# A Perceiver layer pair on one core: another order of loads at the start, another first expert, and causal weights zeroed on GpSimd

## The chip, the core and the metric

The kernel runs on one core of one Trainium2 chip. The metric is the device time of one execution in microseconds. An execution under the profiler has a time of its own, and its span (first to last instruction) is a little shorter than that time.

## The reference

The input is a latent x of 512 tokens by 512 features, a context of 8192 tokens by 512 features, and a mask over the context. Two layers follow each other, and each adds three blocks to x in turn. All have 16 heads of 32 features.

- Cross attention: layer norm of x, queries from it, keys and values from the context, a softmax over the context tokens that the mask leaves, an output projection. In layer 0 queries and keys are normalised per head.
- Self attention over the 512 tokens. In layer 0 a score counts only where the key's position is not before the query's:

```python
scores = jnp.where(j >= i, scores, -jnp.inf)
attn = jax.nn.softmax(scores, axis=-1)
```

  In layer 1 each query sees a window of neighbours.
- A mixture of 8 experts. A router picks two experts for each token, and the gated sum of their answers is added. The hidden width is 2048 in layer 0 and 1024 in layer 1.

## The kernel before, in words

Everything is float32, with small bfloat16 products where a mask or a shift is added to scores. The program is written against a framework that schedules: it gives every DMA one of eight semaphore lanes for each kind of queue in turn, makes a DMA wait until the last user of its lane has landed, and arranges each engine's instructions by when it expects them to be ready. [...]

**Opening.** Constants are built on GpSimd (POOL): masks, counters, and `rooms`, which hold each expert's capacity and first row. The key mask (`c8`) is turned into a short list `irow` of at most 15 context tiles that hold an unmasked token (`tile_list`). SP reads this list into registers (L609) and then issues the context tiles (`cslot`, L620), two to a slot, four slots at once. Ahead of that SP loads x in four pieces, the query weights `wq`, and the broadcast biases `bq` and `bkf`; ACT loads the key and value weights `wkvf` in four pieces. `columns` (L935) loads a vector of 512 numbers as 128 x 4, through ACT's queue; `padded_columns` (L1242) loads a key bias in four pieces, through SP's queue. `columns_of` uses both and scales the query bias on POOL (L943). `clear_answers` writes zeros into `answers_d`, the DRAM buffer for the experts' answers, with nine stores of 256 KB and a small one through POOL's queue (L84, L85). `aside`, called in the fourth step of the key loop, holds the output bias, those zeros and the columns for the next blocks, but the scheduler may issue them earlier.

**Cross attention (layer 0).** Layer norm (`lnt` is its transposition on TensorE), values of four tiles (`pv`), queries (`qps`), and then a loop over the 15 tiles: keys (`pk`), their normalisation, the transposition (`ktp`), running maxima of scores. A scan of the other mask runs beside it: SP loads pieces `mi`, POOL reads the first column of each (`first`), ACT squares differences (`square`). Then a long loop of scores, exponentials and weighted sums, kept ahead by the maxima of the next group of heads.

**Self attention (layer 0).** Four groups of four heads. For each group four steps, from the last block of 128 keys to the first, with 512, 384, 256 and 128 queries. A first pass (`M` in a hand-written order of steps) takes maxima, a second (`W`, function `weighted`) subtracts them by a small product, takes exponentials into `pT`, and `sums` multiplies the last step's `pT` with values (`acc`) and with ones (`den`). In both passes a bfloat16 product of `negi` (minus a huge number on the diagonal) with `before` (one where the key is before the query) is added to the diagonal block of scores (L1314). `F` finishes a group; the last group is finished by query block (`E`, `T`).

**Experts.** Experts are ranked by how many tokens chose them; rank r has room for `CAPS[r]` tokens, and the products for it have that many columns. `by_rank` finds the rank of each expert (`erank`), and `has` marks which expert stands in which place. The loop goes through the places in order, in `n` chunks of 512 hidden features (4 in layer 0, 2 in layer 1): `hidden` (`hps`), the activation, `back` (`y`). SP issues two weights of 1 MB for each chunk, four buffers each. Tokens of the first place are gathered by products with a one-hot matrix (`gather`, `gps`, L1737). For the others, a list of tokens (`lists`, `token_of`) is made and POOL gathers blocks of 128 rows from DRAM (`xrows`, L1751), which TensorE transposes (`xtp`, L1759). The loop asks for the blocks that the second place needs in its chunk before the last of the first place:

```python
if i % n == n - 2 and r + 1 < E:
    while waiting and waiting[0][0] * P < starts[r + 1] + caps[r + 1]:
        waiting.pop(0)[1]()
        fetch()
```

## Time and profile before

| | |
|---|---|
| time, median of 3 runs | 1718.99 us (1718.89 to 1719.83) |
| the profiled execution: its own time | 1715.68 us |
| its span | 1713.8 us |
| mean granted TensorE clock | 0.941 |
| TensorE (PE) busy | 1566.6 us, 91% |
| VectorE (DVE) / ScalarE (ACT) / GpSimd (POOL) busy | 45% / 33% / 25% |
| first value product on TensorE | at 28.24 us |
| causal self attention | about 556 to 650 us |
| experts of layer 0 / layer 1, first product of the gather | at 670.46 us / 1515.61 us |

A line of the timeline gives the start, the duration, the engine, the source line, the operation with output and inputs, and in brackets the engine's idle time before it with what ended it. SPq, ACTq and the like are DMA issues. A line of the windows gives a stretch, then for PE, PEld (TensorE's weight loads), DVE, ACT and POOL the busy time with the count of instructions, then the granted TensorE clock, the share of the DMA engines' time and GB/s. A group has busy time and mean duration, then idle time before it.

### The profile page before, as it was taken

What the parts mean: (1) busy time and instruction counts of PE and PEld (TensorE: products, weight loads), DVE (VectorE), ACT (ScalarE), POOL (GpSimd) and SP (SyncE); (2) the same over time, 40 slices, a digit from 0 to 9 for tenths busy, and PEclk for the clock granted to TensorE, in tenths of its full rate; (3) what the DMA queues carried; (4) which work ended last, traced back from release to release, by engine and by line L of the source; (5) the groups of instructions that cost most, each with busy time, mean ns of one, the idle gap of its engine ahead of it and who ended that gap; (6) DMA issues with size and microseconds to landing.
All of it is one profiled execution on the core that took longest, in us unless ns stands there. A gap on an engine that the chain in (4) does not pass through costs nothing. (4 is left out here: it accounts for less than half of the span.)

```text
span 1713.8 us, 24266 instructions
## 1 busy us (share of the span) xinstructions
PE 1566.6 (91%) x9933; PEld 914.2 (53%) x9933; DVE 775.0 (45%) x1394; ACT 569.5 (33%) x1079; POOL 424.9 (25%) x306
## 2 busy tenths in 40 slices
PE   3889999999979997999999799999999989679996
PEld 2333333333234446999999465433333245369995
DVE  5366677774633645111112233567765536831112
ACT  1366445556622132111111211165556612211110
POOL 4000057788110001000002100068776110010002
PEclk9999989999989977999999899999999989879997
DMA  7055200000030003878885400000000040064672
GB/s 247 24 161 178 74 1 1 1 1 1 1 129 1 1 1 134 311 265 286 282 295 171 155 25 19 25 1 1 1 1 1 1 151 10 15 224 171 219 265 90
DMA packets 87144, 168.79 MB, mean 98 GB/s; under 512 B 8450, under 2 KB 23842, under 8 KB 85600
## 3 DMA queue, kind: packets, MB, share of 16 engines
q1 hardware_dynamic: 78352, 147.87, 25.4%
q0 software_dynamic: 5440, 17.01, 2.8%
q10 hardware_dynamic: 3216, 2.11, 0.4%
q8 instruction: 84, 1.38, 0.3%
q14 instruction: 52, 0.43, 0.1%
HBM read 156.30 MB, written 9.63 MB: 97 GB/s over the span
## 5 line engine op out<-in xcount | busy, mean ns | idle before, releaser
L869 ACT ACTIVATE pT<-sc,kbias 128x512 f32<-128x512 f32 x480 | 299.1, 686 | 205.1 <-PE sc L639 142.4
L752 PE MATMUL sc<-qTf,kTf 32*128 32x512 f32 x1264 | 297.0, 653 | 6.4 <-DVE d L861 4.9
L765 DVE SCALAR_TENSOR_TENSOR mx<-scm,kbias,mx 128x512 f32<-128x512 f32 x312 | 215.4, 743 | 97.8 <-PE scm L752 95.5
L752 PE MATMUL scm<-qTf,kTf 32*128 32x512 f32 x656 | 240.8, 653 | 2.1 <-DVE mx L765 2.1
L1790 PE MATMUL y<-hT,w 128*128 128x160 f32 (+13 forms) x1536 | 212.3, 298 | 2.4 <-DVE hT L1965 2.3
L1790 PEld LDWEIGHTS y<-hT,w 128*128 128x128 f32 x1536 | 205.1, 197 | 4.4 <-DVE hT L1965 2.8
L1774 PE MATMUL hps<-tokens,w 128*128 128x160 f32 (+13 forms) x1536 | 207.0, 293 | 0.0
L1774 PEld LDWEIGHTS hps<-tokens,w 128*128 128x128 f32 x1536 | 198.7, 192 | 1.8
L842 POOL TENSOR_TENSOR four<-four,pT 128x2048 f32<-128x2048 f32 x42 | 190.6, 4538 | 9.7 <-ACT pT L869 6.7
L752 PEld LDWEIGHTS sc<-qTf,kTf 32*128 32x128 f32 x1264 | 90.6, 189 | 148.4 <-issue 111.9
L842 POOL TENSOR_TENSOR four<-pT 128x2048 f32<-128x2048 f32 x24 | 109.0, 4542 | 109.2 <-ACT pT L869 109.2
L824 PE MATMUL acc<-pT,vNf 128*32 128x512 f32 x960 | 133.8, 624 | 1.5 <-ACT o L831 1.5
L765 DVE SCALAR_TENSOR_TENSOR mx<-sc,kbias,mx 128x512 f32<-128x512 f32 x136 | 93.3, 744 | 79.8 <-PE sc L752 79.8
L1965 DVE TENSOR_TENSOR hT<-sg,hps 128x320 f32<-128x320 f32 (+7 forms) x64 | 27.9, 436 | 189.5 <-ACT sg L1964 189.5
L752 PEld LDWEIGHTS scm<-qTf,kTf 32*128 32x128 f32 x656 | 75.0, 188 | 49.8 <-DVE mx L765 38.0
L639 PE MATMUL sc<-shift,ones 3*128 3x512 bf16 (+3 forms) x544 | 100.2, 383 | 0.0
L1815 POOL DMA_DIRECT2D answers_d<-yb x17 | 9.4, 556 | 291.7 <-ACT yb L1808 291.7
L1964 ACT ACTIVATE sg<-hps 128x320 f32<-128x320 f32 (+7 forms) x64 | 25.3, 396 | 135.1 <-PE hps L1774 135.1
L1012 PE MATMUL pv<-wkvf,cslot 128*128 128x512 f32 x120 | 56.8, 617 | 13.3 <-DMA cslot<-in_ctxT 13.2
L824 PEld LDWEIGHTS acc<-pT,vNf 128*32 128x32 f32 x960 | 20.7, 109 | 87.7 <-issue 80.5
L653 DVE TENSOR_REDUCE neg<-mtp 128x4 f32<-128x512 f32 x64 | 41.2, 683 | 55.7 <-PE mtp L650 55.7
L1690 POOL DMA_DIRECT2D tokens_d<-xn x8 | 4.5, 569 | 241.3 <-issue 143.5
(331 smaller groups left out, 1844.5 us busy)
## 6 DMA issues: line engine op xcount, KB each, us to landing
w<-in_L_ffn_W SPq DMA_DIRECT2D x96, 1024.0 KB, 7.6
mi<-in_mask SPq DMA_DIRECT2D x32, 512.0 KB, 4.3
cslot<-in_ctxT SPq DMA_DIRECT2D x30, 256.0 KB, 4.3
answers_d<-yb POOLq DMA_DIRECT2D x15, 256.0 KB, 7.2
answers_d<-zero POOLq DMA_DIRECT2D x9, 256.0 KB, 3.2
wkvf<-in_L_xattn_WkvT ACTq DMA_DIRECT2D x4, 512.0 KB, 6.4
wq<-in_L_xattn_WqT SPq DMA_DIRECT2D x2, 1024.0 KB, 7.8
wof<-in_L_xattn_WoT SPq DMA_DIRECT2D x2, 1024.0 KB, 4.7
```

Source lines behind the costliest of these rows:

```text
L639: nc.tensor.matmul(ps, lhsT=ones16[r, :], rhs=k.shifts[g][r, 0:w], start=start, stop=stop)
L653: nc.vector.tensor_reduce(neg[:, h, :], tp.rearrange("p (t k) -> p t k", k=P), AX.X, ALU.max, negate=True)
L752: nc.tensor.matmul(ps, lhsT=kT[HD * h : HD * (h + 1), g, i * P : (i + 1) * P], rhs=qT[HD * h : HD * (h + 1), g, :], start=True, stop=stop,)
L765: nc.vector.scalar_tensor_tensor(to, ps, b, to, ALU.add, ALU.max)
L824: nc.tensor.matmul(k.sums[g][HD * h : HD * (h + 1), :], lhsT=vN[:, i, g * P + HD * h : g * P + HD * (h + 1)], rhs=pT[:, h, :], start=(i == ...
L842: engine.tensor_tensor(to, parts[g][-1], pT, ALU.add)
L869: nc.scalar.activation(pT[:, h, :], ps, AF.Exp, bias=kbias[:, i : i + 1])
L1012: last = nc.tensor.matmul(ps.rearrange("p (g n) -> p g n", g=NG), lhsT=src[:, c, s % 2, :], rhs=wkv[:, :, c, i * P : (i + 1) * P], start=( ...
L1774: nc.tensor.matmul(ps[:, j, 0:k], lhsT=w1[:, c, f * P : (f + 1) * P], rhs=tokens[:, c, starts[r] : starts[r] + k], start=(c == 0), stop=(c ...
L1790: nc.tensor.matmul(accs[0][:, d, 0:k], lhsT=w2[:, f, d * P : (d + 1) * P], rhs=hT[:, f, 0:k], start=(c == 0 and f == 0 and d % 2 == 0), st ...
L1964: nc.scalar.activation(sg, ps, AF.Sigmoid)
L1965: nc.vector.tensor_tensor(dst, sg, ps, ALU.mult)
```

## The change

Four edits. First, `columns` and `padded_columns` issue on GpSimd instead of ACT and SP. Second, the load of the output bias moves into `aside`, and what `aside` holds is put in a block that binds its instructions behind the last of the first four value products, as far as they are on that product's engine. Third, the capacities and the ranks are put in the order 4, 0, 1, 2, 3, 5, 6, 7, so that the first place holds the expert of rank 4 (132 instead of 160 tokens in layer 0, 112 instead of 256 in layer 1). Fourth, the second pass of the causal attention no longer adds the masking product; after the exponentials, one GpSimd instruction for each step writes zero where the key is before the query. The first pass keeps its masking product.

```diff
-CAPS0 = (160, 152, 148, 140, 132, 124, 116, 112)
-CAPS1 = (256, 224, 192, 160, 112, 96, 64, 48)
+RANKS = (4, 0, 1, 2, 3, 5, 6, 7)
+CAPS0 = (132, 160, 152, 148, 140, 124, 116, 112)
+CAPS1 = (112, 256, 224, 192, 160, 96, 64, 48)
...
+    ranks = const.tile([P, E], F32, name="ranks")
+    for r in range(E):
+        nc.gpsimd.memset(ranks[:, r : r + 1], float(RANKS[r]))
...
     def columns(pool, vector, tag):
-        nc.scalar.dma_start(out=t, in_=vector.rearrange("(g p) -> p g", p=P))
+        nc.gpsimd.dma_start(out=t, in_=vector.rearrange("(g p) -> p g", p=P))
...
-            nc.gpsimd.dma_start(out=bo, in_=a["L0_xattn_bo"].partition_broadcast(P))
...
             def aside():
-                add_bias(bo)
-                clear_answers(qp)
-                columns_of("L0_attn")
-                columns_of("L1_xattn")
+                with tc.issue_after(valued.ins):
+                    nc.gpsimd.dma_start(out=bo, in_=a["L0_xattn_bo"].partition_broadcast(P))
+                    add_bias(bo)
+                    clear_answers(qp)
+                    columns_of("L0_attn")
+                    columns_of("L1_xattn")
...
     def padded_columns(pool, src, tag):
-            nc.sync.dma_start(
+            nc.gpsimd.dma_start(
...
-                if shifted:
-                    for h in range(GH):
-                        k.subtract(g, h, tiles[h][:, 0:w], w, stop=False)
                 for h in range(GH):
-                    nc.tensor.matmul(tiles[h][:, w - P : w], lhsT=negi, rhs=before, start=False, stop=True)
+                    if shifted:
+                        k.subtract(g, h, tiles[h][:, 0:w], w)
+                    else:
+                        nc.tensor.matmul(tiles[h][:, w - P : w], lhsT=negi, rhs=before, start=False, stop=True)
...
                     nc.scalar.activation(pT[:, h, 0:w], tiles[h][:, 0:w], AF.Exp)
+                nc.gpsimd.affine_select(
+                    out=pT[:, :, w - P : w], in_=pT[:, :, w - P : w], compare_op=ALU.is_ge, fill=0.0,
+                    base=0, pattern=[[0, GH], [-1, P]], channel_multiplier=1,
+                )
                 sums()
...
-            has, erank.unsqueeze(1).to_broadcast(sq), number.unsqueeze(2).to_broadcast(sq), ALU.is_equal
+            has, erank.unsqueeze(1).to_broadcast(sq), ranks.unsqueeze(2).to_broadcast(sq), ALU.is_equal
...
-                k = min(S, 2 * S // (r + 1)) - caps[r]
+                k = min(S, 2 * S // (RANKS[r] + 1)) - caps[r]
```

The last line is in `rest`, which runs only when an expert has more tokens than its place.

## The prediction

> **What bounds the kernel now.** I read the page first, then the waits and the timeline of the three stages that the diff touches, then windows of two microseconds for the clock.

> ```profile
> span 1713.8 us, 24266 instructions
> PE 1566.6 (91%) x9933; PEld 914.2 (53%) x9933; DVE 775.0 (45%) x1394; ACT 569.5 (33%) x1079; POOL 424.9 (25%) x306
> ```

> TensorE is busy for 91% of the span, so a gain is either PE work taken away or PE idle time closed. The first idle stretch is the longest, and the opening's timeline says what it waits for:

> ```profile
> 12.19 0.33 SPq L973 DMA_DIRECT2D bkf<-in_L_xattn_bkv  x1
> 14.06 4.86 SPq L1242 DMA_DIRECT2D L_attn_bk<-in_L_attn_bkT  x4
> ...
> 18.15 4.88 POOL L84 DMA_DIRECT2D answers_d<-zero  x9
> ...
> 18.95 0.61 SPq L1242 DMA_DIRECT2D L_xattn_bk<-in_L_xattn_bkT  x1
> ...
> 21.64 1.10 DVE L189 TENSOR_SCALAR xn<-x,ln_m,ln_r 128x512 f32<-128x512 f32 x2
> ...
> 23.97 6.26 SPq L620 DMA_DIRECT2D cslot<-in_ctxT  x8
> 28.24 3.75 PE L1012 MATMUL pv<-wkvf,cslot 128*128 128x512 f32 x4 [13.17 <-DMA cslot<-in_ctxT]
> ...
> 31.79 1.66 PE L192 MATMUL lnt<-ident,xn 128*128 128x128 f32 x8
> ```

> The list of context tiles (irow) is written on DVE at 9.62 us, but SP, which issues in order, puts five tiny column loads ahead of reading it. The first context tile is issued at 23.97 and TensorE idles until 28.24. Two other places matter: the masking products in the causal attention, and the wait for gathered tokens at the start of the second experts layer.

> ```profile
> L1314 PE MATMUL sc<-before,negi 128*128 128x128 bf16 x80 | 9.8, 237 | 0.0
> ...
> 590.60 0.23 PE L1314 MATMUL sc<-before,negi 128*128 128x128 bf16 x1
> ...
> 591.65 0.40 PE L1338 MATMUL acc<-pT,vNs 128*32 128x128 f32 x8
> ...
> 1515.61 9.94 PE L1737 MATMUL gps<-at,xn 128*128 128x256 f32 x32 [3.64 <-DVE erow L1566]
> ...
> 1537.45 0.63 PE L1759 MATMUL xtp<-ident,xrows 128*128 128x128 f32 x4 [3.21 <-DMA xrows<-tokens_d,token_of]
> ...
> 1539.60 8.14 PE L1774 MATMUL hps<-tokens,w 128*128 128x256 f32 x32
> ```

> **The change part by part.** (1) *Opening.* Removed from SP's queue ahead of the list: the five loads, 14.06 to 19.56. Removed from ACT's queue: five column loads, which hide anyway (ACT's first other work starts at 15.3). In the built order of the changed kernel SP goes from bkf straight to the list. bkf itself waits for the semaphore lane of an x piece: before, the fourth (5.0 us in SP's waits), now the second; x pieces are issued from 1.22 on and land a median 7.7 us later, so bkf goes out near 9. Reading the list took 4.1 us (SP's entry L609): 9.65 + 4.1, first context tile issued near 13.9, 10.1 us earlier. It does not pay 10.1. First, the tile lands 4.0 us after issue at best: 18.0. Second, SP's ring still holds wq, bq and bkf, which landed at 14.9 to 17.5. Third, the zeros come earlier, not later: the built order puts nothing on POOL behind the value product, since the block's ordering binds only instructions of that product's own engine. On POOL the zeros no longer wait for the two scaled bias columns (issued 16.67 and 17.94), only for lanes that free from about 12.5, so nine stores of 256 KB start near 12.8 instead of 18.15.

> ```profile
> 10.00:15.00 5.00, 0.16 (x1) 0.18 (x1) 0.95 (x4) 0.00 (x0) 0.16 (x1) 1.00 1.04 377
> 15.00:20.00 5.00, 0.07 (x1) 0.00 (x0) 5.00 (x13) 1.69 (x3) 2.32 (x6) 1.00 0.64 111
> 20.00:25.00 5.00, 0.00 (x0) 0.00 (x0) 4.27 (x10) 0.00 (x0) 3.53 (x7) 1.00 0.97 366
> ```

> (columns: PE, PEld, DVE, ACT, POOL busy, granted clock, DMA share, GB/s.) The 16 engines are full from 10 to 15, have room from 15 to 20, and then carry the zeros. [...] by the rows the sequencer time is 5.5 us of SP plus an earlier read of the list, with a 0.64 share open just there. I follow the rows[...]: sharing about 380 GB/s with the zeros I put it at 19.5 (18.0 free; 24.2 if all 2.36 MB of zeros went first, 6.2 us). Two half-clock products (2.7 us, 28.24 to 30.94) end near 22.3. Next late is DVE: lnt needs xn of 21.64 to 22.74, which hangs on wq's landing at 14.89; with wq 0.5 to 1 us later lnt starts at 23.5 to 24 against 31.79. So 8.0 us (4.8 to 9.5). What follows (the list of chains up to the main loop) is PE, DVE and ACT work of the same order and moves along; the mask's pieces wait for products and squares, not for a clock time. The moved columns: 13 on POOL, each 0.5 to 1 us to issue by its 0.5 to 0.75 us rows, at most double for 512 four-byte pieces; they queue ahead of POOL's reads of the mask's first column until about 45 us. ACT's squares wait for those; only the first two pairs run before the later context slot is freed (80.5 us before), so nothing. Eight extra memsets: 8 x 0.035 us of issue, ahead of DMAs that land before they are used: nothing.

> (2) *Causal weights.* Of the 80 products counted, 64 in all go from the second pass (16 steps of 4; the other 64 in the maxima stay). The 237 ns is a latency; the pace is the start to start: a step of four costs 0.33 us at full clock and 0.50 at half. 64 products are 11 x 0.33 + 5 x 0.50 = 6.1 us. Added: 16 selects on POOL, idle in this stage (0.00 busy from 560 to 650), over 4 x 128 columns. Its rows are 0.23 us for 64 columns and 0.28 for 128; along that slope 0.61 for 512, in proportion 1.13, and POOL's 128x512 TENSOR_SCALAR is 1.57. I take 0.75, nearest to the slope. It stands between the last exponential and the products with the values, and those queue behind it on PE. The order leaves one step of scores between them, except at the end of groups 0 to 2: there 128-column weights are used 1.05 us after their scores (590.60 to 591.65), while exponential (0.96) plus select plus two hand-overs of 0.15 need about 2.0. Three stalls of 0.8 to 1.0 us, less a few transposes that the new order puts in front. 6.1 - 2.6 = 3.5, of which 0.5 is lost where PE waits for DVE anyway (2.6 us on neg, 1.8 on x). So 3.0 us gained (6 gained to 1.5 lost).

> (3) *First expert.* The same eight capacities in another order, so the big products sum to the same, and so do the weights. What differs is the head. Layer 1: gps with 112 columns instead of 256. The clock is 0.50 until 1521 in both, where a product costs about 0.22 instead of 0.33 us: it ends near 1522.2 instead of 1525.5, and the token list 3.1 us later (layer 0's uninterrupted chain, 676.99 to 680.12), 1525.4 instead of 1529.9. But hps for 112 columns covers only 3.6 us instead of 6.9, and three gathered blocks are needed ahead of y instead of two ahead of hps: the third lands about 9.4 us after the list. PE stalls from about 1529 to 1535 and is through the transposes at 1535.4, against 1539.6, with 3.3 us more of product work and one more block (0.6) left: 0.3 us gained. Layer 0 (160 to 132): the same reckoning gives 0. [...] The rows show that the shorter stalls of before already paid:

> ```profile
> 1534.00:1536.00 2.00, 0.24 (x2) 0.00 (x0) 0.69 (x1) 0.60 (x1) 1.20 (x2) 1.00 1.04 385
> ...
> 1538.00:1540.00 2.00, 1.36 (x6) 1.25 (x6) 0.00 (x0) 0.74 (x2) 0.94 (x1) 0.58 1.03 383
> ```

> A stall of 3.2 us was followed by 0.58. So I take 0.3 us lost for both layers (1.5 gained to 4 lost). Two more gathers of 0.95 us on POOL in layer 1 find it idle.

> **Sum.** -8.0 - 3.0 + 0.3 = -10.7 us on the profiled execution: span 1713.8 to 1703.1, its own time 1715.68 to 1705.0. The median of the runs shown stands 3.3 us above that execution; I carry the difference over: 1718.99 - 10.7 = 1708.3.

> **The rivals.** (a) As summed, 60%: 1708.3, own range 1704 to 1712. (b) The zeros crowd the context: DMA at 1.04 up to 15 us speaks for it; SP's transfers kept landing 0.9 us apart while other stores ran, against. Opening 4.8: 1711.5; 12%. (c) The select becomes the new wait: 1.13 us or more, and every step's products late; attention at 0: 1711.3; 12%. (d) The clock helps: PE's 2.6 us idle at 594.9 was followed by 17 us at half speed:

> ```profile
> 594.00:596.00 2.00, 0.85 (x7) 0.48 (x5) 2.00 (x1) 0.00 (x0) 0.00 (x0) 1.00 0.00 0
> ...
> 598.00:600.00 2.00, 2.00 (x8) 1.20 (x6) 2.00 (x10) 0.00 (x0) 0.00 (x0) 0.50 0.00 0
> ```

> With that stretch gone, 8.5 us: 1700; 6%. (e) The other side, slower: [...] Each new 17 us stretch costs 8.5 us; the kernel is slower once more than 21 us of half clock are added; two stretches give 1725, one gives 1717. 10%, of which 6 slower. That the zeros are not later is no rival but counted in (1).

> **How the numbers follow.** A measurement of this kernel tells 0.2% (3.4 us) from no change. Faster is (a) to (d) less 3% for (b) and (c) together with a stretch: 0.87; within 0.2%: 0.07 (those 3% and the 4% of (e) with one stretch); slower: 0.06. 1701 to 1715 takes in (b), (c) and a small part of (d), and leaves out about 15%.

> **What would show it.** First cslot issue at 13.9 and pv at 19 to 20; zeros from about 12.8; lnt near 24. No L1314 under the second pass, selects of 0.6 to 1.1 us, PE waits on POOL at three places. In layer 1 an xtp wait of 5 to 6 us, gps ending 3 us earlier. I am wrong if the first tile lands past 23, if selects exceed 1.5 us, or if the clock rows of 556 to 650 gain a half-speed stretch.

## The result, and the profile after

The changed kernel takes 1699.26 us (median of 4 runs, 1697.87 to 1702.98) against 1718.94 us for the kernel before (4 runs, 1717.58 to 1719.83): a ratio of 0.989, 95% interval 0.9872 to 0.9907, or 19.7 us less. The forecast was 10.7 us less, 1708.3 us with a range of 1701 to 1715. The direction was right; the time lies below the range. The spans of the two profiled executions differ by less, 1713.8 to 1698.5, that is 15.3 us.

The page after begins:

```profile
span 1698.5 us, 24206 instructions
PE 1559.3 (92%) x9877; PEld 908.3 (53%) x9877; DVE 775.3 (46%) x1394; ACT 570.7 (34%) x1081; POOL 446.5 (26%) x345
```

TensorE is busy 7.3 us less and idle 8.0 us less. The opening's timeline answers to the one shown of before:

```profile
10.39 0.75 POOL L156 DMA_DIRECT2D router<-in_L_ffn_router  x1 [4.46 <-issue]
11.67 6.79 SPq L625 DMA_DIRECT2D cslot<-in_ctxT  x8
13.50 0.52 POOL L981 DMA_DIRECT2D nrows<-in_L_xattn_kn_b  x1
16.66 1.08 POOL L86 DMA_DIRECT2D answers_d<-zero  x2
19.93 0.24 PE L999 MATMUL nwp<-ident,nrows 4*128 4x4 f32 x1 [10.92 <-DMA nrows<-in_L_xattn_kn_b]
20.21 3.46 PE L1016 MATMUL pv<-wkvf,cslot 128*128 128x512 f32 x4
24.62 1.18 PE L197 MATMUL lnt<-ident,xn 128*128 128x128 f32 x8 [0.95 <-DVE xn L194]
```

The first value product comes at 20.21 us, 8.0 earlier than before, as forecast. But `pv` has no wait of its own: the context tile, issued at 11.67, had landed at 17.04. TensorE stood at `nwp`, the transposition of the norm rows, which is ahead of it in the queue. These rows were late because POOL stood still for 4.46 us ahead of its first load, with no wait recorded (`<-issue`).

In the causal stage the selects appear, with those who waited for them (us, times):

```profile
L1356 POOL TENSOR_SCALAR_AFFINE_SELECT pT<-pT x16: 637/637/729, 540.1 to 635.0; 128x512 f32<-128x512 f32 x16
  PEld acc L1344: 2.1, 4
  PEld accq L1379: 0.8, 1
  PE acc L1344: 0.2, 1
```

637 ns each (0.75 us forecast), and about 3 us of waits for them. The stage as a whole, from the first causal scores to the first product of the gather, first in before and then in the changed kernel, as windows (columns: length, busy time of PE, PEld, DVE, ACT, POOL with counts, granted clock, DMA share, GB/s):

```profile
508.59:670.46 161.87, 146.53 (x1040) 75.06 (x1039) 82.75 (x195) 40.66 (x97) 2.29 (x5) 0.87 0.02 7
```

```profile
505.94:659.98 154.04, 135.61 (x975) 67.52 (x975) 82.83 (x195) 40.90 (x97) 12.54 (x20) 0.89 0.02 8
```

It is 7.8 us shorter, where the forecast had 3.0. And TensorE in the second experts layer:

```profile
1500.67 5.68 PE L1748 MATMUL gps<-at,xn 128*128 128x112 f32 x32 [3.56 <-DVE erow L1577]
...
1510.01 5.43 PE L1785 MATMUL hps<-tokens,w 128*128 128x112 f32 x32
1516.84 0.63 PE L1770 MATMUL xtp<-ident,xrows 128*128 128x128 f32 x4 [1.39 <-DMA xrows<-tokens_d,token_of]
1518.00 0.84 PE L1770 MATMUL xtp<-ident,xrows 128*128 128x128 f32 x4 [0.53 <-DMA xrows<-tokens_d,token_of]
1519.29 1.08 PE L1770 MATMUL xtp<-ident,xrows 128*128 128x128 f32 x4 [0.44 <-DMA xrows<-tokens_d,token_of]
```

The gather takes 4.3 us less than before, and the stall for gathered blocks is 2.4 us in three pieces, not 5 to 6 in one.

**A reading used below.** From each trace I take TensorE's busy time (the union of its products) and the stretches of half clock, in which the granted clock is 0.50. Half of the busy time inside these stretches is called the *loss*; busy time less the loss is the *work* at full clock; the rest of the length is *idle*. So a length is work + idle + loss. The loss is an estimate, since it takes every product to last twice as long at half clock; that the work comes out alike under different losses (123.4 and 123.0 us under 12.2 and 16.2) speaks for it. The clock is on record from 33.06 us on in before and from 23.24 in the changed kernel; half clock ahead of that is not counted. The three parts of the change in the three profiles of before and two of the changed kernel:

| | to first `pv` | `pv` to last `ktp` (half clock in it) | causal stage = work + idle + loss | layer 0 experts | layer 1 experts to the end |
|---|---|---|---|---|---|
| before | 28.24 | 160.6 (6.8) | 161.9 = 129.1 + 15.3 + 17.4 | 287.6 | 198.2 |
| before, second | 29.01 | 161.5 (6.8) | 161.6 = 129.1 + 15.2 + 17.4 | 284.7 | 197.6 |
| before, third | 28.04 | 158.7 (3.4) | 161.9 = 129.1 + 15.4 + 17.5 | 284.8 | 198.0 |
| changed | 20.21 | 165.9 (17.1) | 154.0 = 123.4 + 18.4 + 12.2 | 284.2 | 197.8 |
| changed, second | 19.80 | 162.1 (3.4) | 154.1 = 123.4 + 18.5 + 12.2 | 284.6 | 197.1 |

(Layer 0 experts: first product of the gather to layer 1's first `lnt`. Parts of a sum are rounded singly.) Between the means of these rows the five stretches change by -8.4, +3.8, -7.8, -1.3 and -0.5 us; all else adds 1.0, and the span is 13.2 us shorter.

### The profile page after: what moved, and what is told of

The parts are those of the page before. It is cut to its first block, busy times and chain, and to the rows that moved or that the text cites. A ratio compares the mean times of both kernels' runs of the same rounds, so it can differ in the third digit from the quotient of the medians.

```text
span 1698.5 us, 24206 instructions
## 1 busy us (share of the span) xinstructions
PE 1559.3 (92%) x9877; PEld 908.3 (53%) x9877; DVE 775.3 (46%) x1394; ACT 570.7 (34%) x1081; POOL 446.5 (26%) x345
## 5 line engine op out<-in xcount | busy, mean ns | idle before, releaser
L1801 PE MATMUL y<-hT,w 128*128 128x112 f32 (+13 forms) x1536 | 211.0, 297 | 0.6 <-DVE hT L1976 0.6
L1785 PE MATMUL hps<-tokens,w 128*128 128x112 f32 (+13 forms) x1536 | 208.5, 295 | 0.0
L1976 DVE TENSOR_TENSOR hT<-sg,hps 128x264 f32<-128x264 f32 (+7 forms) x64 | 28.0, 437 | 189.5 <-ACT sg L1975 189.5
L1975 ACT ACTIVATE sg<-hps 128x264 f32<-128x264 f32 (+7 forms) x64 | 25.4, 397 | 137.4 <-PE hps L1785 137.4
L1981 DVE TENSOR_TENSOR hT<-sg 128x224 f32<-128x224 f32 (+7 forms) x32 | 14.7, 459 | 107.6 <-ACT sg L1980 107.6
```

Source lines behind the costliest of these rows:

```text
L1785: nc.tensor.matmul(ps[:, j, 0:k], lhsT=w1[:, c, f * P : (f + 1) * P], rhs=tokens[:, c, starts[r] : starts[r] + k], start=(c == 0), stop=(c ...
L1801: nc.tensor.matmul(accs[0][:, d, 0:k], lhsT=w2[:, f, d * P : (d + 1) * P], rhs=hT[:, f, 0:k], start=(c == 0 and f == 0 and d % 2 == 0), st ...
L1976: nc.vector.tensor_tensor(dst, sg, ps, ALU.mult)
```

## The experiments

All kernels of a group ran on one chip beside runs of before. "Span times clock" is the span multiplied by the mean granted clock; it leaves out most of how much half clock an execution drew. Of before, 83 timed runs came together, those of the first comparison included: mean 1716.8 us, 1707.5 to 1724.2.

| run | what it is | median, us | ratio to before (95%) |
|---|---|---|---|
| e1 | opening alone | 1703.88 | 0.9927 (0.9904 to 0.9949) |
| e2 | causal edit alone | 1711.30 | 0.9975 (0.9956 to 0.9994) |
| e3 | order of experts alone | 1716.91 | 1.0001 (0.9985 to 1.0016) |
| e5 | opening and causal | 1698.41 | 0.9901 (0.9872 to 0.9931) |
| e6 | causal and experts | 1707.11 | 0.9948 (0.9927 to 0.9968) |
| e7 | changed kernel again | 1702.11 | 0.9921 (0.9896 to 0.9947) |
| e4 | changed, memsets on VectorE | 1704.19 | 0.9915 (0.9885 to 0.9944) |
| e16 | e4 with zeros held back | 1700.77 | 0.9911 (0.9885 to 0.9938) |
| e9 | e5 with all mask products kept | 1705.32 | 0.9939 (0.9911 to 0.9967) |
| e10 | e5 with a quarter of them kept | 1701.24 | 0.9913 (0.9886 to 0.9939) |
| e11 | changed, 15 idle products in the key loop | 1699.81 | 0.9913 (0.9884 to 0.9942) |
| e12 | changed, idle products in the router | 1703.44 | 0.9927 (0.9904 to 0.9950) |
| e13 | changed, 6 idle products in the key loop | 1696.60 | 0.9891 (0.9858 to 0.9923) |
| e14 | e13 and idle products in the router | 1697.13 | 0.9878 (0.9845 to 0.9911) |
| e17 | e13 and e16 together | 1693.54 | 0.9870 (0.9846 to 0.9894) |

**One edit at a time (e1, e2, e3).** The theory was the prediction's sum; the rival put the surplus into half clock. Each kernel is before with one hunk of the diff: `columns`, `padded_columns`, `aside` in e1; `weighted` and `scores` in e2; `RANKS` and capacities in e3.

> The kernel before with the opening edits alone (column loads and padded column loads on GpSimd, output bias and zeros in the bound block). Sum of the prediction: 8.0 us less than before (4.8 to 9.5), and all of it is still there at the end. Rival, the clock grid: in the profile of the full change the first value product comes 8.0 us earlier, but of this only 2.7 us is left at 160 us, because three half-clock windows (10.2 us) more fall between 60 and 145 us; by that this kernel is 3 to 5 us faster and shows 5 to 12 us more of half clock ahead of 160 us. Second question: in the full change GpSimd stands still from 5.9 to 10.4 us without any wait, then issues the rows for the norms late; they land at 19.8 and hold the first value product at 20.2, though its context tile has landed at 17.0. If the eight extra memsets for the ranks moved a boundary of instruction fetching in front of these loads, this kernel has no such gap, and its first value product starts near 17.2; if the gap comes from the opening edits, it is here too, and the product starts near 20.

> The kernel before with the causal edit alone (selects on GpSimd in place of the 64 mask products of the second pass). Sum of the prediction: 3.0 us less. Reading of the changed profile: about 4.1 us less in the stage itself and up to 3.4 us less through two half-clock windows fewer between 590 and 665 us, so 4 to 7.5 us. Rival, the surplus of the change lies elsewhere: 2 to 3 us.

> The kernel before with the order of experts alone. Sum of the prediction: 0.3 us more than before (1.5 less to 4 more). Reading of the changed profile: layer 0 gains nothing at its head but 3.7 us at its end (the last expert's wait for its activation is 0.6 instead of 2.3 us, and a half-clock window behind it is gone), layer 1 gains 1 to 2 us: 4 to 6 us less. Rival, the gain at the end of layer 0 came from the earlier stages: 0 to 2 us. If the eight extra memsets cost an instruction fetch, GpSimd has a gap of about 4.5 us near 6 us here as well, with little harm, as the context comes at 28 us.

Between means the opening takes 12.5 us less (1704.4 to 1716.9), the causal edit 4.8 less, the order of experts 0.8 more. So the order of experts is worth nothing clear of the scatter, as forecast, and the opening is worth more than its 8.0 (by its interval 8.8 to 16.5 us). The causal mean is above its 3.0 too, but its interval, 1.0 to 7.6 us, takes 3.0 in. In span times clock the three are 8.2, 2.4 and 1.3 us less, so the opening without clock is near the forecast. The profile of e1 has 10.2 us more of half clock in the key loop than the first of before (17.1 to 6.8), as the rival had it, but the timed runs do not show the smaller gain that it expected. e2's causal stage took 157.5 us (123.0 + 18.4 + 16.2): work and idle as in the changed kernel, but a loss of 16.2 instead of 12.2.

**In pairs, and again (e5, e6, e7).** In span times clock the three alone gave 12 us and the whole change 16.6, so I asked whether they help each other.

```text
e5: opening + causal hunks, capacities and ranks as before
e6: causal hunks + capacities and ranks, opening as before
e7: the changed kernel, unaltered
```

> The changed kernel without the order of experts: opening and causal edits on the kernel before. Alone, the three edits came to 12.5, 4.3 and 0.2 us by the ratios; in span times mean clock, which leaves out how much half clock an execution drew, they came to 8.2, 2.5 and 1.3 us (12.0 together), while the whole change came to 16.6 us. Theory of additive edits: 10.7 us less than before in span times clock, some 15 us in time, and the order of experts is worth about 1 us more. Theory of interaction: the order of experts is worth more once the stages ahead are shorter, so this kernel stays near 10.7 us in span times clock and the changed kernel is 5 to 6 us faster than it. Third: opening and causal edits help each other, then this kernel is at 15 to 16 us already.

> The changed kernel without its opening edits: causal edit and order of experts on the kernel before. Additive: 3.8 us less than before in span times clock. Interaction of these two: 8 us less. If the missing 4.6 us come with the opening: 3.8 us here.

> The changed kernel once more, unaltered. If the first comparison (19.7 us between medians of four runs each) drew a slow set of runs of before and a fast set of the changed kernel, the difference is now 15 to 18 us, and span times clock is again 1592 us within 1 us; if it was typical, 19 to 20 us.

Between means e5 is 16.9 us below before, e6 9.4, e7 14.5; in span times clock 13.5, 7.4 and 14.7. e5 lies between the theories and cannot separate them. e7 shows that the first comparison drew well: the changed kernel's 10 runs average 1701.2 us, 15.6 below the 83 of before. A least-squares fit of three additive parts to the seven differences between means (12.5, 4.8, -0.8, 16.9, 9.4, 14.5, and 19.0 of the first comparison) gives opening 11.0, causal 6.0, experts 0.5 us less, each with a standard error of about 1.7; no difference misses the fit by more than 3.0 us. Interaction is not needed, but the scatter would hide one of 2 or 3 us.

**The kernel before again (e8, e15).**

> The kernel before once more, unaltered, for a second profile. The profile of before had a span times clock of 1612.7 us where its 26 timed runs average 1608.6. If single profiles differ by some 4 us from what is typical, this one shows another set of half-clock windows (another phase of the 3.41 us grid) and shorter idle stretches at 935 us; if the profile was typical, the same windows to within a few us.

> The kernel before once more, for a third profile. Its two profiles lose 101 us of span to half clock (span less span times clock), its 57 timed runs 105 on average, between 96 and 114. If the two drew low by chance, this one loses more, and shows where: most likely a longer half-clock stretch between 480 and 510 us (10.2 us there so far, 23.9 in the kernel with the causal edit alone) or in the key loop. If it shows 101 again, executions with a profile differ from the others.

The profiled executions took 1715.68, 1710.98 and 1708.44 us; all three lose 101 us of span by the clock, against 105 on average in the timed runs. The wait at the end of layer 0's experts, 2.3 us in the first profile, is 1.6 and 1.7 in the other two. I expected a third profile to show where typical executions lose 4 us more; it did not. So the spans of profiles (before 1709.8 on average, changed 1696.6) differ by 13.2 us where the timed runs differ by 15.6, and where the rest sits stays open.

**GpSimd's standstill (e4, e16).** The eight memsets of the ranks had been costed at nothing.

```diff
e4:
-        nc.gpsimd.memset(ranks[:, r : r + 1], float(RANKS[r]))
+        nc.vector.memset(ranks[:, r : r + 1], float(RANKS[r]))
e16, also:
-        nc.gpsimd.memset(zero, 0.0)
+        nc.gpsimd.tensor_scalar(zero, behind, 0.0, None, ALU.mult)
...
-                    clear_answers(qp)
+                    clear_answers(qp, vN[:, 0, :])
```

> The changed kernel with its eight extra memsets on VectorE instead of GpSimd, nothing else. If the gap of GpSimd at 5.9 to 10.4 us is an instruction fetch whose boundary the memsets moved ahead of the loads of the norm rows: the gap moves behind these loads, they land near 15 us, the first value product starts at about 17.2 instead of 20.2 us, and the kernel gains up to 3 us on the changed one (ratio to before about 0.987). If the gap has another cause: it stays, and the kernel equals the changed one (0.989). If layer norm's inputs come too late to use an earlier value product, the product starts earlier but the gain is under 1 us.

> The changed kernel with its eight extra memsets on VectorE (as in the fourth experiment) and with the zeros held back by data: the tile of zeros is made from the first tile of values, so that no store of zeros can start before the first context tile has been used. In the changed kernel the first context tile lands at 17.0 us and the norm rows, late from GpSimd's standstill at 5.9 to 10.4 us, hold the first value product to 20.2; with the memsets on VectorE there is no standstill, but the zeros start at 12.9 and the tile lands at 21.6. If both causes are as read: norm rows by 15, tile by 17.3, first value product at 17 to 17.5, layer norm's transpositions next (they wait for VectorE until about 22), 2 us gained at that point. If the tile is slow for another reason (registers, its own packets), it lands at 18.5 or later and the gain is under 1 us.

Timelines of e1, which lacks the memsets, and then of e4:

```profile
13.25 1.22 POOL L84 DMA_DIRECT2D answers_d<-zero  x2 [0.55 <-DMA router<-in_L_ffn_Wg]
...
15.75 0.24 PE L994 MATMUL nwp<-ident,nrows 4*128 4x4 f32 x1 [6.76 <-DMA nrows<-in_L_xattn_kn_b]
...
19.15 3.75 PE L1011 MATMUL pv<-wkvf,cslot 128*128 128x512 f32 x4 [3.17 <-DMA cslot<-in_ctxT]
```

```profile
12.94 3.52 POOL L86 DMA_DIRECT2D answers_d<-zero  x6 [0.53 <-DMA router<-in_L_ffn_Wg]
...
14.90 0.23 PE L999 MATMUL nwp<-ident,nrows 4*128 4x4 f32 x1 [5.91 <-DMA nrows<-in_L_xattn_kn_b]
...
21.86 3.75 PE L1016 MATMUL pv<-wkvf,cslot 128*128 128x512 f32 x4 [6.73 <-DMA cslot<-in_ctxT]
```

Neither kernel has the standstill ahead of POOL's loads; e3 and e6, which have the memsets on POOL but not the opening edits, have it too (5.04 and 4.47 us). So the memsets bring it there: shown. With it gone the norm rows come by 15, but the zeros start at 12.9 instead of 16.7 and the context tile lands at 21.6 instead of 17.0. The standstill had held the zeros back. e4 gains nothing in time. Its late tile is not typical, though: in e1, e5, e9 and e10, also without the memsets, the zeros start just as early (13.0 to 13.3), and the tile lands at 18.9 to 19.6. Holding the zeros back by data as well brings `pv` to 18.77, with the tile landing at 18.5 (18.6 in e17), not 17.3: the lesser branch of what was expected, and within the scatter in time. So holding the zeros back brings the tile 0.3 to 1.1 us forward against those four kernels and 3.0 to 3.1 against e4. The standstill had also held back the 256 KB load of the output bias, issued at 14.79 in the changed kernel and at 9.9 to 10.0 in all kernels without the memsets that have the opening edits; whether that is the rest was not tested.

**Work, waits or clock in the causal stage (e9, e10).** Both build on e5.

```diff
+                keep = shifted and True          # e10: and g == NG - 1
                 for h in range(GH):
                     if shifted:
-                        k.subtract(g, h, tiles[h][:, 0:w], w)
-                    else:
+                        k.subtract(g, h, tiles[h][:, 0:w], w, stop=not keep)
+                if keep or not shifted:
+                    for h in range(GH):
                         nc.tensor.matmul(tiles[h][:, w - P : w], lhsT=negi, rhs=before, start=False, stop=True)
```

> Opening and causal edits (the kernel of the third experiment's group, without the order of experts) with the 64 mask products of the second pass kept beside the selects: the work of before and the waits of after together. In the profiles so far the stage from the first causal scores to the first product of the gather takes 161.6 to 161.9 us with products alone (129.1 of work, 15.3 idle, 17.4 lost to half clock) and 154.0 to 154.2 with selects alone (123.4, 18.4, 12.2) in five profiles of six. If work and waits add up and the clock follows neither: 129 + 18.4 + 12 to 17, so 160 to 165 us. If the 5 us of clock come from the removed work (a shorter stage meets the grid of windows otherwise): the loss is back at 17, so about 165 us, and the kernel is some 10 us slower than without the products. If they come from the selects themselves (other idle stretches): 12, so about 160 us, 6 us slower.

> The same, but the mask products are kept beside the selects in the last of the four groups only: 16 products, 1.4 us of work just ahead of the stage's tail (layer norm, router). By work alone the stage takes 155.4 us. By the grid of windows the tail arrives 1.4 us later in its window; two idle stretches of 1.9 and 1.4 us, which lay half in one window and half in the next (busy shares 0.53 and 0.51 in the changed kernel, no half clock), then fall into one window, the tail runs at half clock 7 us longer, and the stage takes 158 to 159 us.

| causal stage | length = work + idle + loss |
|---|---|
| e5, selects alone | 154.0 = 123.4 + 18.4 + 12.2 |
| e10, 16 products kept | 157.6 = 124.1 + 18.0 + 15.4 |
| e9, 64 products kept | 160.7 = 127.9 + 17.0 + 15.8 |

In e9 most of the removed work is back (4.5 of 5.7 us) and most of the clock loss with it (3.6 of 5.2). By the loss this is nearer to the first of the two clock branches; by the length, 160.7, and by the 6.2 us between the means of e9 and e5 it is at the second, so e9 does not decide between them. e10 is the sharper one: 0.7 us of work brought 3.2 us of loss. The windows show how, first in the changed kernel, then in e10 at the same place (columns as above):

```profile
641.00:645.00 4.00, 2.16 (x10) 1.15 (x10) 2.72 (x9) 0.34 (x1) 0.68 (x2) 1.00 0.02 4
645.00:649.00 4.00, 3.63 (x27) 3.24 (x27) 1.36 (x6) 2.12 (x7) 1.56 (x3) 0.86 0.54 214
649.00:653.00 4.00, 3.00 (x15) 2.90 (x14) 0.93 (x5) 1.34 (x2) 0.00 (x0) 0.50 0.12 48
```

```profile
634.00:638.00 4.00, 1.38 (x4) 0.61 (x5) 2.72 (x10) 0.00 (x0) 0.00 (x0) 0.91 0.00 0
638.00:642.00 4.00, 4.00 (x20) 3.66 (x18) 2.21 (x9) 1.36 (x4) 1.71 (x4) 0.50 0.35 131
642.00:646.00 4.00, 4.00 (x20) 3.78 (x20) 0.00 (x0) 1.54 (x3) 0.53 (x2) 0.50 0.36 131
```

After the same two idle stretches (1.9 and 1.4 us) the changed kernel stays at full clock for 4 us more, while layer norm begins; e10 falls to half at once. In time e10 is 1 us above e5 (means), which is within the scatter, so its 3.6 us longer stage is seen in one profile of each.

**Filling the waits (e11, e12, e13, e14, e17).** The question was whether products without use in TensorE's waits keep the clock at full speed.

```diff
                 tp = psum.tile([P, NG, P], F32, name="ktp", tag="s")
+                for _ in range({2: 5, 8: 3}.get(s, 0)):          # e13: 2 and 1
+                    nc.tensor.matmul(tp, lhsT=ident, rhs=wkv[:, :, 0, 0:P], start=True, stop=True)
...
                         tp = psum.tile([P, NG, P], F32, name="qtp", tag="s")
+                        for _ in range(7 if t == 2 else 0):      # e13: 3
+                            nc.tensor.matmul(tp, lhsT=ident, rhs=wkv[:, :, 0, 0:P], start=True, stop=True)
e12: 3 such products ahead of pos and 4 ahead of gps (e14: 1 and 2)
```

> The changed kernel with 15 idle products (7, 5 and 3 of 128x128 by 512 columns, 0.43 us each, results overwritten) where TensorE waits 3.8, 3.1 and 2.4 us in the key loop: behind the third block of queries, and ahead of the transpositions of the third and ninth key tile. If half clock there (3.4 to 17 us, up to 7.5 us lost in the profiles) comes from windows less than half busy: no half clock between 55 and 145 us, and the stretch from the first value product to the last key transposition takes 158 us instead of 162 to 166; the kernel gains 3 to 6 us on the changed one. If the clock does not answer to such work: no gain, and 0.5 us lost where a product outlasts the wait.

> The changed kernel with seven idle products in each layer's router chain: three ahead of the counts, four between the counts and the gather, where TensorE waits 2.8 to 4.0 and 3.6 us for VectorE. In the profiles the gather runs at half clock (6.3 us in layer 0, 5.7 in layer 1), and in layer 1 the lists and the first products as well. If busy windows bring the clock back, gather and first products run at full clock: 2.5 us gained in layer 0 and up to 4 in layer 1. If the clock comes back only after the products are over (each takes 0.86 us at half clock, and one window must pass): they outlast the waits by up to 0.5 us and nothing is gained.

> The changed kernel with 6 idle products (3, 2 and 1) in the three waits of the key loop, where the run before had 15: each takes 0.9 us, twice what I had reckoned, so those outlasted the waits (work 12.4 us up, idle time only 9.4 us down). If the clock is decided by windows less than half busy, half clock between 55 and 145 us is 0 to 3.4 us, the idle products lie inside the waits, and the stretch from the first value product to the last key transposition takes 158 to 159.5 us (162.1 and 165.9 in the two profiles of the changed kernel): 3 to 5 us gained on its pooled mean of 1701.6 us. If fewer products leave the windows under half busy: no difference.

> The same, and in each layer's router chain one idle product ahead of the counts and two ahead of the gather, where the run before had three and four. If they bring the clock back in time, the gather of layer 0 ends 2 us and the first products of layer 1 up to 4 us earlier than in the kernel beside it; if the clock needs a fully busy window of 3.4 us first, which two products at half clock give only as the gather begins, under 1.5 us in all.

> Both: zeros held back and memsets on VectorE, and the six idle products in the key loop. If the two gains stand side by side, the last key transposition comes at 174.5 to 175.5 us (176.9 with the idle products alone, 181.9 and 186.1 in the two profiles of the changed kernel), and the kernel's mean is 1693 to 1696 us. If an earlier opening meets the grid of windows otherwise, half clock of 3.4 to 7 us comes back in the key loop and the mean is 1697 or more.

The key loop, from `pv` to the last `ktp`, in the changed kernel and then in e13, as windows:

```profile
20.21:186.07 165.86, 145.86 (x444) 63.20 (x444) 97.46 (x183) 81.64 (x194) 24.18 (x52) 0.95 0.42 132
```

```profile
19.96:176.94 156.98, 143.89 (x455) 62.77 (x456) 97.23 (x183) 81.93 (x194) 23.41 (x52) 1.00 0.45 140
```

No half clock is on record there in e11, e13 and e17, and one window of 3.4 us in e14, which has the same six products; the fifteen profiles with these waits unfilled have 3.4 to 17.1. In e13 the stretch is 157.0 us, 5.2 and 8.9 shorter than in the two profiles of the changed kernel; e14 and e17 have 158.5 and 156.7, and no unfilled kernel with the opening edits is under 159.4. TensorE is even busy for less time, useless products included. e11 gave most of that away because each product takes 0.9 us, twice what I had reckoned: work up 12.4 us, idle down 9.4; its mean, 1701.2, is that of the changed kernel. e13's mean is 1696.9 us, 4.3 below the changed kernel's ten runs, with a standard error of 1.8 on the difference; e17's, with the zeros held back too, 1694.3, the best here (0.987) and within what was expected of it. In the router chain the filling gained nothing, neither in e12 nor on top of e13 in e14.

## Why the prediction was right and wrong

The step that failed is in part (2): it put the effect of the clock on the causal stage at nothing. The profiles show 5.2 us less loss there, more than the 2.6 us of its direct terms. A second surplus, some 3 us that the timed runs give to the opening, has no cause that the runs show.

**Opening, forecast 8.0.** Right at the first value product (8.0), and right in span times clock (8.2 in e1), but in the changed kernel not by its steps. The 8.0 was worked out for layer norm's transpositions, and these start 7.2 us earlier (24.62 instead of 31.79). `bkf` went out at 9.22, as reckoned, but reading the list took 1.6 us (L614) where 4.1 had been carried over from before. So the tile was issued at 11.67, not 13.9, and landed at 17.0, not 19.5, which was my estimate. The wait that ended last was the norm rows, through the memsets that I had costed at nothing; that the first product still came when forecast is luck, two errors that cancel. Without the standstill, in e1, e5, e9 and e10, the tile lands at 18.9 to 19.6 and `pv` starts at 19.2 to 19.9, close to the reckoning. Rival (b), the zeros crowding the context, shows in e4 alone (21.6).

"Two half-clock products (2.7 us, 28.24 to 30.94)" misreads its line, which has four, to 31.99 (0.85 us from start to start, against 0.43 from 33.29 on); nothing hung on it, as `lnt` waits for `xn` in the changed kernel. "What follows moves along" is in doubt: the key loop is 161.1 us on average in six profiles without the opening edits (158.7 to 163.8), 163.1 in nine with them (159.4 to 165.9; those with its waits filled left out), which would be 2 us given back, most of it as half clock; but the ranges overlap. In the timed runs the opening is nevertheless worth 11 us; that the profiles of before sit low is part of it, the rest is open.

**Causal weights, forecast 3.0: this step failed.** Its direct terms were right. Work fell by 5.7 us (6.1 forecast), idle rose by 3.1 (2.6 of stalls and 0.5 lost to VectorE forecast), the selects took 0.64 us: 2.6 net. The term left at zero was the clock: the loss fell from 17.4 to 12.2 us, and the stage by 7.8 in all. I had it as rival (d), at 6% and tied to one place, the 17 us stretch at 597; that one only went to 13.7, and more came from the tail (23.9 to 17.1 us of half clock). It is not a constant: e2, with the same edit, kept a loss of 16.2, and e11 one of 16.1. With 5.2 us added, the forecast would have been 1703.1. That is a saving of 15.9 us, beside the 15.6 of all runs; the agreement is in part luck, since the fit of the timed runs gives the causal edit 6.0 and the opening 11.0.

**First expert, forecast 0.3 lost.** Right as a sum (e3: ratio 1.0001), wrong in its pieces. The 0.6 us between the 0.3 gained by the reckoning of products and the 0.3 lost were my estimate for the clock. In the first profile of each, layer 1 has 2.0 us less work, 0.9 less idle and 2.5 more loss (12.4 to 14.9; 11.6 and 13.2 in the other two of before, 14.2 in the second of the changed kernel): its head runs at half clock in part (granted 0.65 over `gps`, 0.69 over `hps`), so that `hps` took 5.43 us, where I had reckoned 3.6, and hid the blocks that I let TensorE stall for.

**The base.** I carried the 3.3 us between the profiled execution and the median over unchanged. Single executions of before spread over 17 us, most of it clock: within the groups, span times clock varies by 1.7 to 3.0 us (standard deviation) where the time varies by 3.4 to 5.5. A part of the first difference of 19.7 us is such a draw; 15.6 is the better number.

## What to carry to other kernels

Sum work, idle time and clock loss separately, stage by stage: here 0.7 us of kept work in the causal stage went with 3.2 us of loss (e10 against e5), so give that term its own bounds instead of zero. Before trusting a difference of under 1%, profile the same kernel twice more, and compare times together with span times clock. Where TensorE waits 2 to 4 us again and again, try useless products cut to fit the wait: they gained about 4 us in the key loop and nothing in the router chain. Measure the length of one first.

## What the runs showed of the hardware

**Where the causal stage began.** The causal stage of the kernels without the edit (before, e8, e15, e1, e3) began 0.83 to 1.25 us into a window in all five profiles (1.08 in before) and took 161.6 to 161.9 us. With the selects, no products kept and the router chain as it was, it began at 1.19 to 1.55 in eight profiles (1.42 in the changed kernel; 153.9 to 154.2 us), and at 0.76 and 0.90 in two, e11 and e2 (157.4 and 157.5). So the edited stage took one of two times, about 3.4 us apart. Why these starts lie so close together was not tested.

**A standstill that no wait explains.** POOL stopped at about 6 us in the kernels with eight more instructions ahead of its loads (for 4.46 us in the changed kernel, 5.04 in e3, 4.47 in e6), while the 16 DMA engines were full (in the changed kernel the two large queues had 55 and 50% of their time from 6 to 11 us). The trace has one packet on the instruction queue then (8.5 us in the changed kernel); but before and e1, which do not stand still there, have one as well (9.1 and 9.9). So whether POOL waited for instructions stays open; that the memsets bring the standstill about was shown.
